# Moving two small parameter loads to an earlier joint, and regrouping the row loads of the last stage

## The chip, the cores and the metric

The kernel runs on one core of one Trainium2 chip, in one launch. The metric is the device time in microseconds (us), as a median over runs. Engines are named as the profile names them: PE (TensorE matmuls) and PEld (its weight loads), DVE (VectorE), ACT (ScalarE), POOL (GpSimd) and SP (SyncE), which computes nothing here and issues most DMAs.

## The reference

Two layers, each a graph attention over a dense 0/1 adjacency matrix followed by a mixture of experts, on 2708 rows of 256 features in float32. What the change touches is the end of layer 1:

```python
def _L1_ffn_ref(x, gate_w, gate_b, w1, b1, w2, b2, gamma, beta):
    gate_logits = x @ gate_w + gate_b                # 16 experts
    topk_vals, topk_idx = jax.lax.top_k(gate_logits, 2)
    topk_w = jax.nn.softmax(topk_vals, axis=-1)
    h = jax.nn.relu(jnp.einsum('bsh,ehf->bsef', x, w1) + b1)
    expert_out = jnp.einsum('bsef,efh->bseh', h, w2) + b2
    sel = jnp.take_along_axis(expert_out, topk_idx[..., None], axis=2)
    y = x + jnp.sum(topk_w[..., None] * sel, axis=2)
    mu, var = jnp.mean(y, -1, keepdims=True), jnp.var(y, -1, keepdims=True)
    return (y - mu) / jnp.sqrt(var + 1e-5) * gamma + beta
...
x = x + _L1_gnn_ref(_layernorm(x), adj, 1, L1_gnn_W_gcn, L1_gnn_W_att, L1_gnn_a_att)
x = x + _L1_ffn_ref(_layernorm(x)[None], ..., L1_ffn_gamma, L1_ffn_beta)[0]
```

gamma and beta are vectors of 256 numbers.

## The kernel before

**Tiles.** The rows are cut into 22 tiles: 20 full ones of 128 rows and two of 74 (`tiles`, `TF`, `TAIL`).

**Stages.** Attention 0 and experts 0 come first, then the preparation of layer 1, attention 1 (its matmuls L1638 run from 719.5 to 872 us), the stream of experts 1 (its last matmul ends at 1112.5 us) and a last stage. Attention 1 and experts 1 are not two loops. `attention`, `points1`, `scatter1`, `experts1.stream` and others are generators, and a planner (`Clock`) with estimated costs lets each emit its next instructions when it thinks that the engine is free. The planner sets the order in which each engine gets its instructions when the kernel is built; on the chip each engine goes through its own list in order and waits for semaphores. `clock.moved(mark, us, latency)` only tells the planner how long a transfer is thought to take.

**The joint behind attention 1.** When the last attention matmul is emitted, `attention` closes the pool `att1`, and calls `late_pools`, which opens the pool `gamma_beta` in the room that `att1` has left and the third set of weight buffers (`room2`). Then SP's list has the loads of experts 1.

**Experts 1.** The router scatters every token's row to two places in a DRAM table `rows_d` (L674, indirect DMAs of POOL), so that rows of one expert lie in pages of 128. `stream` then goes through 45 blocks of 128 rows (`SURE1`). For each block SP issues three DMAs: `load_w1` (L749, 512 KB) and `load_w2` (L753, 512 KB) into one of three buffer sets, and `fetch` (L765, 129.5 KB: the block's rows). A weight load is skipped at run time when the set holds that expert already; the profile then shows it with 0.07 to 0.09 us in place of 0.37 or more. PE runs the matmuls L880 into `hid_ps` (16 by the profile's count), ACT the relu, PE the matmuls L898 into `out_ps` (8), DVE weighs (L904), and POOL adds the block's rows to one of two DRAM tables, `sums1[b % 2]`, by an indirect DMA that accumulates (L909). So even blocks go to table 0 and odd ones to table 1, and block 44, the last, goes to table 0.

`experts1.beside` is `add_beta(b)`, called behind each block. At block 16 it loads gamma and beta, each as one row of 256 numbers repeated over 128 partitions (`broadcast_rows`, L228); from block 20 on it starts one `add_to_x` per block, which adds beta to the rows of `x1` (DVE L1926).

**Early last stage.** `early_last` does the last normalisation of tiles 0 to 5 and 6 to 11 while the stream's final blocks run: it loads both tables' rows (L1420), adds them on POOL (L1953), takes mean and variance on DVE (L427, L428), and applies gamma and the rest (DVE L1963, L1965).

**Last stage.** Behind the stream stands `experts1.rest()`, a conditional block for pages beyond 45, which this input does not enter; its instructions are at L940 and L943. Then `load_y` fetches the rows of `tiles[12:14]`, `[14:16]`, `[16:20]` and `[20:22]` from both tables; `early_out` stores tiles 6 to 11 (L1974); and `last1` does the same sums and normalisation for the late tiles: POOL L1990, DVE L427 and L428, ACT for the root, DVE L2003 and L2005, and the stores L2008. `fetch_rows` issues one DMA for the full tiles of a group (L1420) and one for tiles of 74 rows (L1423).

Of the kernel before, what the change touches and what calls it, by code (L numbers as in the profile page):

```python
# [146 lines left out]
def kernel(  # L147
# [25 lines left out]
    nc = tc.nc  # L173

    ctx.enter_context(tc.manual_schedule(engines={ET.PE, ET.Activation, ET.DVE, ET.SP}))
    N, D = x.shape
# [16 lines left out]
    SURE0, SURE1 = 47, 45  # L193
# [32 lines left out]
    def broadcast_rows(name, src, offset, n, queue=nc.gpsimd, pool=const):  # L226
        tl = pool.tile([P, n], F32, name=name)
        queue.dma_start(  # L228
            tl, bass.AP(tensor=src.tensor, offset=src.offset + offset, ap=[[0, P], [1, n]])
        )  # L230
        return tl
# [275 lines left out]
    def sums_d(name, zero=False):  # L507

        t = dram.tile([W + P, D], F32, name=name)
        lo = 0 if zero else T  # L510
        nc.sync.dma_start(t[lo * P:, :].rearrange("(t p) d -> p t d", p=P),
                          nobody[:, :D].unsqueeze(1).to_broadcast([P, T + 1 - lo, D]))
        return t
# [816 lines left out]
    for step in range(START + T * len(pairs)):  # L1330
# [15 lines left out]
        if step >= START:  # L1346
            k, j = divmod(step - START, T)
# [67 lines left out]
    def fetch_rows(tl, src, group):  # L1415

        full = [t for t, r in group if r == P]
        if full:
            lo = full[0] * P
            ins = nc.sync.dma_start(tl[:, :len(full)], src[lo:lo + len(full) * P, :].rearrange(  # L1420
                "(t p) d -> p t d", p=P))
        if len(full) < len(group):
            ins = nc.sync.dma_start(tl[:TAIL, len(full):], src[TF * P:W, :].rearrange(  # L1423
                "(t p) d -> p t d", p=P)[:TAIL])
        return ins
# [224 lines left out]
    last = pairs[AHEAD - 1]  # L1650
# [5 lines left out]
    for k in range(17):  # L1656
# [8 lines left out]
        if k >= 14:  # L1665
            lo = 4 * (k - 14)
# [25 lines left out]
    sums1 = [sums_d(f"sums1_{k}", zero=k == 1) for k in range(2)]  # L1692
# [11 lines left out]
    clock = Clock()  # L1704
# [34 lines left out]
    def attention():  # L1739
        for i in range(2, T):  # L1740
            acc_slots[i] = yield from acc.get()
            accs[i] = ps_tile("att_ps", "acc")
            for part in range(2):
                yield wide_at[i, part]
                for j in range(part, T, 2):
                    yield "PE", 0.265
                    sum_up(i, j)
                clock.set(wide_slots[i, part])
            clock.start(finish1(*tiles[i]), 0)
        att_scope.close()  # L1750
        late_pools()
        clock.set(started)
# [156 lines left out]
    experts1_scope, last = ExitStack(), {}  # L1909

    def late_pools():
        last["pool"] = ctx.enter_context(tc.tile_pool(name="gamma_beta", bufs=1))
        experts1.pool = experts1_scope.enter_context(tc.tile_pool(name="experts1", bufs=1))
        room = experts1.pool.tile([P, 4 * D * 2], F32, name="room2")
        experts1.add_room(2, room[:, :1024], room[:, 1024:])

    def add_beta(b):
        if b == 16:
            for name, src in (("gamma", L1_ffn_gamma), ("beta", L1_ffn_beta)):
                last[name] = broadcast_rows(name, src, 0, D, nc.sync, last["pool"])  # L1920
        if 20 <= b < 20 + T:
            clock.start(add_to_x(*tiles[b - 20]), 3)

    def add_to_x(t, r):
        yield "DVE", 0.47
        nc.vector.scalar_tensor_tensor(x1[:r, t, :], x1[:r, t, :], common[:r, t:t + 1],  # L1926
                                       last["beta"][:r], op0=OP.add, op1=OP.add)


    y_all = mask_flat.bitcast(F32)[:, :2 * T * D].rearrange(  # L1930
        "p (k t d) -> p k t d", k=2, d=D)
# [40 lines left out]
    def early_out(group):  # L1972
        for (t, _), _ in zip(group[::2], group[1::2]):
            nc.sync.dma_start(of_pair(out, t), y_all[:, 1, t:t + 2])  # L1974

    def load_y(group, mark):
        lo = group[0][0]
        for k in range(2):
            fetch_rows(y_all[:, k, lo:lo + len(group)], sums1[k], group)
        clock.moved(mark, 0.8 * len(group), 2.0)  # L1980

    def last1(group, y_at):

# [39 lines left out]
    clock = Clock()  # L2023

    nc.scalar.preload_act_table_set(LN_TABLE)
    late_last = [tiles[12:14], tiles[14:16], tiles[16:20], tiles[20:22]]
    loads = [Mark() for _ in late_last]
    for group, mark in zip(late_last, loads):
        load_y(group, mark)
    early_out(tiles[6:12])  # L2030
    for group, mark in zip(late_last, loads):
        clock.start(last1(group, mark))
# [32 lines left out]
```

## Time and profile before

| what | us |
|---|---|
| three runs | 1159.67, 1155.14, 1156.15; median 1156.15 |
| the profiled execution | 1157.12 |
| its span, first to last instruction | 1155.4 |
| PE busy | 1030.2 (89% of the span) |
| DVE busy | 542.2 (47%) |
| ACT busy | 573.1 (50%) |
| POOL busy | 366.2 (32%) |

The profile gives one execution. Its span is 1.7 us below that execution's own time. In a line of the trace in order of time the first number is the start in us from the span's start, the second how long the instruction or the run of merged instructions took; "x16" is a count; in brackets at the end is how long the engine stood idle before it, and what ended that. SP's lines are DMA issues: the time is the issuing, not the transfer.

### The profile page before, as it was taken

Reading aid. Unit: us, or ns where it says so; the run is one execution under the profiler, and the core shown is the slowest. Engines: PE = TensorE matmul, PEld = TensorE weight load, DVE = VectorE, ACT = ScalarE, POOL = GpSimd, SP = SyncE. Lnnn points to the kernel's source line nnn. Section 1 sums busy time; section 2 is a strip of 40 time slices with the busy share of each in tenths; the row PEclk is TensorE's granted clock in tenths of the full one; section 3 lists DMA queues with packets and bytes.
Section 4 is the critical chain, followed back from the end, with each engine's and each line's share of the span. In section 5 each row is a group of like instructions: output and inputs, shape, how many; then the busy total and the mean of one; then the engine's idle time right before and its main releaser. Section 6 shows DMA issues by size and latency. Waiting matters only on the chain. (4 is left out here: it accounts for less than half of the span.)

```text
span 1155.4 us, 21226 instructions
## 1 busy us (share of the span) xinstructions
PE 1030.2 (89%) x6665; PEld 914.1 (79%) x6665; DVE 542.2 (47%) x2083; ACT 573.1 (50%) x1599; POOL 366.2 (32%) x417
## 2 busy tenths in 40 slices
PE   5999999997999999999999998998984888899850
PEld 3888888875789999999998954998984777798840
DVE  7678888865531111101111336647776641122368
ACT  4876667653534444444443458446753543344420
POOL 7521121111142221112223351252434355333441
PEclk9999999998999999999999999998996899899985
DMA  9965445410898999999899959401125477787973
GB/s 281 288 236 174 156 159 182 135 77 28 295 283 263 322 322 327 324 304 321 250 318 332 335 155 256 153 1 38 60 65 186 122 180 187 171 214 176 282 196 120
DMA packets 165053, 238.96 MB, mean 207 GB/s; under 512 B 10627, under 2 KB 139966, under 8 KB 162224
## 3 DMA queue, kind: packets, MB, share of 16 engines
q1 hardware_dynamic: 146116, 214.09, 56.6%
q0 software_dynamic: 18816, 23.42, 10.6%
q8 instruction: 56, 0.92, 0.3%
q14 instruction: 65, 0.53, 0.1%
HBM read 205.54 MB, written 54.99 MB: 225 GB/s over the span
## 5 line engine op out<-in xcount | busy, mean ns | idle before, releaser
L904 DVE TENSOR_SCALAR yo<-out_ps,w 128x256 f32<-128x256 f32 x92 | 44.5, 484 | 409.4 <-PE out_ps L898 408.8
L1238 PE MATMUL att_ps<-g_all,z 128*128 128x257 f32 (+3 forms) x968 | 227.3, 388 | 0.0
L1238 PEld LDWEIGHTS att_ps<-g_all,z 128*128 128x128 f32 (+3 forms) x968 | 177.3, 188 | 36.3 <-issue 8.9
L898 PE MATMUL out_ps<-room,ht 128*128 128x256 f32 x872 | 200.0, 381 | 0.0
L880 PEld LDWEIGHTS hid_ps<-xt,room 128*128 128x128 f32 x1504 | 176.2, 193 | 6.3 <-issue 3.4
L880 PE MATMUL hid_ps<-xt,room 128*128 128x128 f32 x1504 | 177.5, 277 | 3.2 <-DMA room<-in_L_ffn_W_dram 2.7
L898 PEld LDWEIGHTS out_ps<-room,ht 128*128 128x128 f32 x872 | 161.9, 191 | 21.0
L1224 ACT ACTIVATE zr<-e_bc,minus_one,g_all 128x256 f32<-128x256 f32 (+3 forms) x242 | 130.5, 591 | 59.0 <-DVE z L1227 58.3
L884 ACT ACTIVATE ht<-hid_ps,w_t 128x128 f32<-128x128 f32 x376 | 128.8, 364 | 26.7 <-PE hid_ps L880 7.4
L909 POOL DMA_INDIRECT sums<-yo,xg x43 | 66.8, 1555 | 233.7 <-DVE side L872 204.7
L674 POOL DMA_INDIRECT rows_d<-xr,place x88 | 92.3, 1049 | 123.7 <-DVE xr L443 77.0
L1638 PE MATMUL att_ps<-half,wide_mask 128*128 128x258 f32 (+1 forms) x968 | 124.5, 290 | 2.5 <-ACT h_all L1575 1.5
L1638 PEld LDWEIGHTS att_ps<-half,wide_mask 128*128 128x128 f32 (+1 forms) x968 | 121.5, 195 | 3.9 <-ACT h_all L1575 2.4
L909 POOL DMA_INDIRECT sums<-yo,xr x45 | 70.7, 1572 | 128.9 <-DVE w L902 42.7
L1227 DVE SCALAR_TENSOR_TENSOR z<-zr,mask_t 128x256 f32<-128x256 f32 (+3 forms) x242 | 96.2, 419 | 30.6 <-ACT zr L1224 17.5
L884 ACT ACTIVATE ht<-hid_ps,w1x 128x128 f32<-128x128 f32 x180 | 62.3, 363 | 95.7 <-PE hid_ps L880 92.5
L874 ACT ACTIVATE w<-xg,side 128x1 f32<-128x1 f32 x43 | 12.7, 294 | 167.5 <-DVE side L872 167.5
L1515 POOL CAST wide_mask<-mask_t 128x1408 fp32r<-128x1408 fp8e4 x31 | 42.5, 1376 | 101.6 <-PE att_ps L1638 67.5
L880 PE MATMUL hid_ps<-lo,wide_mask 128*128 128x128 f32 x480 | 65.7, 294 | 9.9 <-DMA wide_mask<-in_L_ffn_w_dram 9.0
L880 PEld LDWEIGHTS hid_ps<-lo,wide_mask 128*128 128x128 f32 x480 | 62.6, 206 | 13.7 <-issue 10.9
L898 PE MATMUL out_ps<-wide_mask,ht 128*128 128x256 f32 x240 | 60.8, 399 | 0.0
L461 PE MATMUL tr_ps<-ident,xr 128*128 128x128 f32 (+1 forms) x214 | 38.7, 291 | 24.0 <-DMA xr<-rows_d 15.6
(292 smaller groups left out, 1328.3 us busy)
## 6 DMA issues: line engine op xcount, KB each, us to landing
room<-in_L_ffn_W_dram SPq DMA_DIRECT2D x94, 1024.0 KB
wide_mask<-in_L_ffn_w_dram SPq DMA_DIRECT2D x60, 512.0 KB
room<-in_adj_dram SPq DMA_DIRECT2D x20, 1354.0 KB
room<-in_L_ffn_w_dram SPq DMA_DIRECT2D x30, 512.0 KB
rows_d<-nobody SPq DMA_DIRECT2D x1, 7511.0 KB
rows_d<-nobody SPq DMA_DIRECT2D x5, 1295.0 KB
sums<-nobody SPq DMA_DIRECT2D x2, 2944.0 KB
xr<-rows_d SPq DMA_DIRECT2D x45, 129.5 KB
```

The lines of the kernel that those rows point to most:

```text
L461: nc.tensor.transpose(ps[:, c, :r], src[:, c * P:(c + 1) * P], ident[:r, :r])
L674: ins = nc.gpsimd.indirect_dma_start(out=self.rows_d[:, :], in_=self.rows[t][:r], in_offset=None, out_offset=bass.IndirectOffsetOnAxis(ap= ...
L880: nc.tensor.matmul(ps[:, :P], w1_b[:, c, f * P:(f + 1) * P], xt[:, c, :], start=(c == 0), stop=(c == DC - 1))
L884: nc.scalar.activation(ht[:, f, :], ps[:, :P], self.func, bias=self.bias[:, f, b:b + 1])
L898: nc.tensor.matmul(ps[:, :D], ht[:, f, :], self.rooms[b % 3][1][:, f, :], start=False, stop=(f == self.FC - 1))
L904: nc.vector.tensor_scalar(yo, ps[:, :D], w, None, op0=OP.mult)
L909: ins = nc.gpsimd.indirect_dma_start(out=self.sums[k][:, :], in_=yo, in_offset=None, out_offset=bass.IndirectOffsetOnAxis(ap=self.rows.pop ...
L1224: nc.scalar.activation(zr[:k, :n], e_bc[:k, lo:lo + n], AF.Relu, bias=minus_one[:k], scale=g_all[:k, j, D + 1:D + 2])
L1227: nc.vector.scalar_tensor_tensor(z[:k, :n], zr[:k, :n], 1.0, mask_t[:k, j // 2, lo:lo + n, j % 2], op0=OP.add, op1=OP.mult)
L1238: nc.tensor.matmul(accs[i][:r, :D + 1], z[:k, q * P:q * P + r], g_all[:k, j, :D + 1], start=(j == 0), stop=(j == LAST))
L1515: nc.gpsimd.tensor_copy(m, src)
L1638: nc.tensor.matmul(accs[i][:, :D + 2], wide_masks[i, j % 2][:k, j // 2, :], half_k[:k, j, :], start=(j == 0 and half_k is halves[0]), stop ...
```

## The change

Two edits. First, gamma and beta are loaded by `late_pools`, right when the pool `gamma_beta` is opened, instead of by `add_beta` at block 16; both loads stay on SP. Second, in the last stage the loads of both tables no longer alternate group by group: all four groups of the table that does not get the last block's addition come first (`SURE1 % 2` is 1, so table 1), then all four of table 0. The planner is told 0.4 us per tile instead of 0.8, since the mark is set behind the second half alone.

The lists of PE, DVE, ACT and POOL are the same before and after, in content and in order. SP's list differs in these two places: gamma and beta stand between the last `xr<-x_d` loads of attention 1 and the first `where` read and weight load of experts 1, and the eight row loads of the last stage are in the new order.

```diff
     def late_pools():
         last["pool"] = ctx.enter_context(tc.tile_pool(name="gamma_beta", bufs=1))
+        for name, src in (("gamma", L1_ffn_gamma), ("beta", L1_ffn_beta)):
+            last[name] = broadcast_rows(name, src, 0, D, nc.sync, last["pool"])
         experts1.pool = experts1_scope.enter_context(tc.tile_pool(name="experts1", bufs=1))
...
     def add_beta(b):
-        if b == 16:
-            for name, src in (("gamma", L1_ffn_gamma), ("beta", L1_ffn_beta)):
-                last[name] = broadcast_rows(name, src, 0, D, nc.sync, last["pool"])
         if 20 <= b < 20 + T:
             clock.start(add_to_x(*tiles[b - 20]), 3)
...
-    def load_y(group, mark):
+    def load_y(group, k):
         lo = group[0][0]
-        for k in range(2):
-            fetch_rows(y_all[:, k, lo:lo + len(group)], sums1[k], group)
-        clock.moved(mark, 0.8 * len(group), 2.0)
+        fetch_rows(y_all[:, k, lo:lo + len(group)], sums1[k], group)
...
     late_last = [tiles[12:14], tiles[14:16], tiles[16:20], tiles[20:22]]
     loads = [Mark() for _ in late_last]
+
+    for group in late_last:
+        load_y(group, SURE1 % 2)
     for group, mark in zip(late_last, loads):
-        load_y(group, mark)
+        load_y(group, 1 - SURE1 % 2)
+        clock.moved(mark, 0.4 * len(group), 2.0)
     early_out(tiles[6:12])
```

## The prediction

> **What bounds the kernel now.** I read the slices of the page first: PE is busy 89% of the span, so I looked for places in the second half where PE waits, with the waits of PE from 895 us on. The longest wait of PE in the experts is at 997.6 us, 8 us behind the two loads that the change moves. Stretches of 10 us around it (after each engine's busy time: granted clock, DMA share, GB/s):
>
> ```profile
> 980.00:990.00 10.00, 10.00 (x70) 9.34 (x69) 1.39 (x7) 4.41 (x15) 4.19 (x3) 1.00 0.49 79
> 990.00:1000.00 10.00, 7.65 (x54) 6.70 (x52) 1.94 (x9) 3.64 (x12) 3.09 (x2) 1.00 0.98 220
> 1000.00:1010.00 10.00, 7.91 (x42) 7.61 (x43) 0.67 (x3) 2.94 (x10) 2.23 (x2) 0.66 0.66 203
> 1010.00:1020.00 10.00, 10.00 (x70) 9.33 (x69) 2.12 (x8) 4.42 (x15) 3.96 (x3) 1.00 0.68 154
> ```
>
> Between 990 and 1000 the DMA engines are busy 98% of the time and move only 220 GB/s. The trace in order of time says around what:
>
> ```profile
> 988.95 0.39 SPq L749 DMA_DIRECT2D wide_mask<-in_L_ffn_w_dram  x1
> 989.39 0.46 SPq L228 DMA_DIRECT2D gamma<-in_L_ffn_gamma_dram  x1
> 989.90 0.42 SPq L228 DMA_DIRECT2D beta<-in_L_ffn_beta_dram  x1
> 990.74 0.39 SPq L753 DMA_DIRECT2D wide_mask<-in_L_ffn_w_dram  x1
> ...
> 994.06 0.60 SPq L749 DMA_DIRECT2D wide_mask<-in_L_ffn_w_dram  x1
> ...
> 1002.09 3.75 PE L880 MATMUL hid_ps<-lo,wide_mask 128*128 128x128 f32 x16 [4.45 <-DMA wide_mask<-in_L_ffn_w_dram]
> ...
> 1008.35 1.95 PE L880 MATMUL hid_ps<-lo,room 128*128 128x128 f32 x16
> ```
>
> PE waits 4.45 us for the weights issued at 994.06, and then runs its 16 matmuls in 3.75 us in place of 1.95. The DMA view of 989 to 999 us, 40 slots of 0.25 us, shows the moved loads at work: from 992.25 the rate falls from 303 to 20 GB/s and is back above 180 from 994.75, while the engines are busy 60% or more in every slot. 256 KB (2 x 128 rows of 1 KB, all from the same two rows of DRAM) take about 2.7 us. At 346 GB/s, the rate of the joint below, 256 KB would take 0.8 us.
>
> The new place is the joint:
>
> ```profile
> 872.76 0.36 PE L831 MATMUL where_ps<-sel,page_start 58*128 58x8 f32 x2
> 874.52 0.40 SPq L749 DMA_DIRECT2D wide_mask<-in_L_ffn_w_dram  x1
> ...
> 887.00 3.69 SPq L765 DMA_DIRECT2D xr<-rows_d  x4
> 889.11 0.69 PE L461 MATMUL tr_ps<-ident,xr 128*128 128x128 f32 x2 [12.13 <-DMA xr<-rows_d]
> ```
>
> PE waits 12.13 us for the first fetch, which SP holds until the scatters have landed (SP waited 5.7 us on rows_d). From 877 to 886 the DMA share is 0.96: weights and scatters fill it. Before 877 it is 0.30 and 0.47.
>
> The chain that ended last lies in DVE from 1135 us to the end. Its last stage, with POOL:
>
> ```profile
> 1125.40 1.26 POOL L1990 TENSOR_TENSOR mask_t<-mask_t 128x512 f32<-128x512 f32 x1 [3.93 <-DMA mask_t<-sums]
> 1125.52 1.42 DVE L1965 SCALAR_TENSOR_TENSOR mask_t<-mask_t,rstd_y,h_all 128x256 f32<-128x256 f32 x1
> 1135.51 0.43 DVE L427 BATCH_NORM_STATS2 bn<-mask_t 128x6 f32<-128x256 f32 x1 [0.95 <-DVEq L943]
> 1136.28 1.26 POOL L1990 TENSOR_TENSOR mask_t<-mask_t 74x512 f32<-74x512 f32 x1 [2.53 <-DMA mask_t<-sums]
> ```
>
> POOL has the first late pair's sum at 1126.66, DVE takes it at 1135.51: the row loads are not late, DVE is.
>
> [...] from 1133.2 to 1134.6, with only a 74-row load left, the DMA share is 0.14, about 2 of 16. [...] Here a wait of 4.45 us cost the clock (0.66 in the stretch), and waits of 0.71 to 1.71 us did not (2.02 us for 16). [...] Here DVE L1965 takes 1.42 us beside POOL and 0.48 alone.
>
> **Part 1, gamma and beta leave block 16.** SP saves 0.46 + 0.42 us and gaps: the weight load at 994.06 came 5.11 us after the one at 988.95, whereas elsewhere two consecutive real loads stand 4.13 (1022.87, 1027.00), 4.15 (1046.87, 1051.02) and 4.53 us (1071.39, 1075.92) apart. So it would be issued at 993.1 to 993.5. Those second loads were used 5.28 us after issue (hid at 1032.28, wait 0.71), 4.66 (1055.68, 0.10) and 5.51 (1081.43, 1.32), here 8.03. Without the two transfers the matmuls start at 993.2 + 5.3 = 998.5 in place of 1002.09: 3.6 us (3.1 to 4.4). The wait shrinks to about 0.9 us, so the clock stays: from this hid to the next takes 6.26 us now (1002.09 to 1008.35), 3.92 behind the short wait at 1032.28: 2.3 us more. A third load in a row can wait some tenths (0.90 at 1060.66): minus 0.2. The sum is **5.7 us**. Behind it PE has no wait until 1032, and later waits hang on loads that themselves wait for PE, so the gain is carried to the end.
>
> **Part 2, they enter the joint.** On SP they stand before the `where` read and all loads of experts 1, and wait for the last attention matmul, since their room is the attention's. That matmul ends at 872.0; issuing takes 0.9 us, to about 873.1; SP's next step waits for ACT L835 until 873.6 anyway. So on SP they cost nothing; should PE's signal be late, each us would delay the loads by one. On the DMA engines 2.7 us of work start about 2.4 us ahead of the weights, in the share that is free; what spills over pushes weights, scatters and, behind them, the fetch at 887. I take 0.6 us, with 0 and 3 us as ends (3: no head start and some queueing on top). Nothing can be gained here.
>
> **Part 3, the order of the last loads.** It is meant to let table 1's loads start before the last addition has landed. I expect that it does not. The last addition is issued at 1116.20; SP's wait for the first load (5.6 us, on the addition) ends at 1121.62. But at the end of `rest()` POOL stands in INC_SWDGE_SEM (L943, 1.5 us from 1120.06)[...]. [...] So the eight loads go out from 1121.66 as now. The first pair then needs the fifth load, not the second. Ahead of that stand 512 KB more for all engines (1.9 us at the 270 KB/us at which the second and third groups follow now: 1536 KB between 1125.40 and 1131.09), and on two engines also table 1's two tiles of 74 rows: 74 rows of 1 KB per engine, 3.2 us at 24 GB/s each (48 GB/s in the stretch above). So the first sum starts at about 1131 in place of 1125.40 (1125.4 + 1.9 + 3.2, and 0.5 to 1 for the fifth load itself), then at 1132.5, 1133.8, 1135.0, and the tail at about 1136.9.
>
> That costs DVE little and relieves it: four of its steps between 1125 and 1134.6 (1.42, 1.50, 1.49, 1.48 in place of 0.48) lost 4.0 us to POOL's sums. Without them it is done at 1130.6, with the branch at 1131.5, and now waits for POOL: sums there at about 1132.6 and 1133.9, statistics of 1.1 us per pair to 1135.0, the root's mend 0.5, then eight steps of 0.46, of which some three lose up to 1 us to POOL's last sums: done at 1141.3, now 1142.2. **0.9 us** gained (from 1 lost, with the loads later still, to 2 gained). The rest of the chain is DVE's and stays.
>
> **The sum.** -5.7 + 0.6 - 0.9 = -6.0 us. The profiled execution was 1157.12 (span 1155.4 and 1.7 around it), 1.0 above the median of 1156.15; from the median: **1150.2 us**.
>
> **The rivals.** (1) The weights are short anyway: three loads in a row are more than the DMA engines deliver, and the wait stays near 3 us with its clock loss, as at 972.66 (wait 2.91, 16 matmuls in 3.59, no gamma near). Then only 2.5 us go: 1153.4. Against it: around 972 the router's scatters of the last group ran beside, which the runs at 1022, 1046 and 1071 lack. (2) Slower: in the joint the same two rows, read by all engines at once, run at the slot's worst rate, 20 GB/s, beside the scatters: 256 KB in 13 us, less 2.4 head start, 10.7 on the fetch and so on PE. -6.6 + 10.7: 1160.3. From 6.6 us of delay on it decides against the change. The 2.7 us measured speak against it. (3) Part 3 does what it says: POOL's wait covers less than I think, table 1 comes from about 1119, sums earlier by 2.5 us; DVE is the bound, so some 1 us more at best: 1149. (4) The last stage gains nothing and the joint takes 3 us: 1153.4.
>
> **How the numbers follow.** My forecast has 0.70 (own range 1148 to 1152.5), (1) and (4) 0.17 together, (2) 0.06, (3) 0.07. The range 1147.5 to 1154.5 takes in (1), (3) and (4). A measurement of this kernel tells about 0.5% (5.8 us) from no change, so faster begins at 1150.4, in the middle of my own case: 0.51 faster, 0.44 the same, 0.05 slower.
>
> **What would show it.** Right: no wait over 1.5 us behind block 16 and 16 matmuls in about 2.0 us there; gamma and beta issued at 872 to 873 and the first weight load still at 874.5; the fetch at 887 to 888; table 1's first load still behind INC_SWDGE_SEM; POOL's first L1990 some 9 us behind the first row load (now 1121.66 to 1125.40, 3.7). Wrong: a PE wait of 3 us or more with a slow clock near 998, or a fetch behind 890.

## The result, and the profile after

The kernel after took 1151.09 us as a median of 22 runs (1147.67 to 1157.67), the kernel before 1155.62 beside it (22 runs, 1150.15 to 1161.28). The ratio is 0.9959, with a 95% interval of 0.9944 to 0.9974: 4.7 us less, from 3.0 to 6.5. The profiled execution of the kernel after took 1152.47 us, with a span of 1150.8.

That execution is 2.3 us later than the one of before at the end of attention 1 (874.3 against 872.0 us), ahead of anything that the change touches; such offsets differ from execution to execution. So all times below are compared from the last attention matmul or from the last matmul of the experts. At block 17 the two executions happen to be only 0.2 us apart (989.97 and 989.74 us), so the stretches around it can be laid side by side.

The stretches of 10 us around block 16 (length, then busy time and count of PE, PEld, DVE, ACT and POOL, then granted clock, DMA share, GB/s; a packet counts whole in the stretch where it starts, so a share can pass 1), kernel after:

```profile
980.00:990.00 10.00, 10.00 (x70) 9.33 (x69) 1.33 (x6) 4.64 (x15) 4.64 (x3) 1.00 0.53 84
990.00:1000.00 10.00, 9.10 (x66) 8.33 (x65) 2.00 (x9) 4.15 (x15) 4.47 (x3) 1.00 0.95 271
1000.00:1010.00 10.00, 10.00 (x71) 9.39 (x70) 1.73 (x7) 4.90 (x17) 3.26 (x3) 1.00 0.70 174
```

PE is busy 9.10 and 10.00 us where it was busy 7.65 and 7.91, the clock stays at 1.00, and the DMA engines, busy 95% (98% before), move 271 GB/s where they moved 220. The trace there in order of time:

```profile
989.18 0.39 SPq L749 DMA_DIRECT2D wide_mask<-in_L_ffn_w_dram  x1
...
993.36 0.37 SPq L749 DMA_DIRECT2D wide_mask<-in_L_ffn_w_dram  x1
993.81 1.95 PE L880 MATMUL hid_ps<-lo,wide_mask 128*128 128x128 f32 x16
...
998.72 2.02 PE L880 MATMUL hid_ps<-lo,wide_mask 128*128 128x128 f32 x16 [0.90 <-DMA wide_mask<-in_L_ffn_w_dram]
```

The two weight loads stand 4.18 us apart (5.11 before), the matmuls that wait for the second start 5.36 us after its issue (8.03), behind a wait of 0.90 us (4.45), and take 2.02 us (3.75).

The joint, kernel after:

```profile
874.33 0.34 SPq L228 DMA_DIRECT2D gamma<-in_L_ffn_gamma_dram  x1
874.72 0.47 SPq L228 DMA_DIRECT2D beta<-in_L_ffn_beta_dram  x1
...
876.91 0.40 SPq L749 DMA_DIRECT2D wide_mask<-in_L_ffn_w_dram  x1
...
889.57 2.59 SPq L765 DMA_DIRECT2D xr<-rows_d  x3
891.66 0.69 PE L461 MATMUL tr_ps<-ident,xr 128*128 128x128 f32 x2 [12.35 <-DMA xr<-rows_d]
```

Counted from the last attention matmul, the first weight load comes 2.6 us after it (2.5 before), the fetch 15.3 (15.0), and PE's wait is 12.35 us (12.13). The joint costs 0.2 us. In the two stretches of 2.5 us behind the last attention matmul the DMA engines were partly free before,

```profile
872.00:874.50 2.50, 0.58 (x4) 0.52 (x4) 2.26 (x15) 1.37 (x6) 1.89 (x3) 0.87 0.30 106
874.50:877.00 2.50, 1.87 (x8) 1.78 (x8) 2.33 (x10) 0.66 (x2) 1.89 (x3) 0.50 0.47 72
```

and are fuller after:

```profile
874.30:876.80 2.50, 0.58 (x4) 0.52 (x4) 2.26 (x15) 1.32 (x6) 1.88 (x3) 0.89 0.60 93
876.80:879.30 2.50, 1.86 (x8) 1.77 (x8) 2.33 (x10) 0.70 (x2) 1.90 (x2) 0.50 1.00 89
```

The last stage, kernel after:

```profile
1111.40 1.54 POOL L909 DMA_INDIRECT sums<-yo,xr  x1 [0.89 <-SPq L943]
1112.41 4.27 POOL L1952 TENSOR_TENSOR mask_t<-mask_t 128x512 f32<-128x512 f32 x3
1114.28 0.43 DVE L427 BATCH_NORM_STATS2 bn<-mask_t 128x6 f32<-128x256 f32 x1 [5.87 <-POOL mask_t L1952]
1116.65 1.42 SPq L1420 DMA_DIRECT2D mask_t<-sums  x3
1127.44 4.92 POOL L1987 TENSOR_TENSOR mask_t<-mask_t 128x512 f32<-128x512 f32 x4 [10.76 <-DMA mask_t<-sums]
1128.73 0.43 DVE L427 BATCH_NORM_STATS2 bn<-mask_t 128x6 f32<-128x256 f32 x1 [2.93 <-POOL mask_t L1987]
```

The first row load comes 5.25 us behind the issue of the last addition, right when POOL's INC_SWDGE_SEM ends at 1116.68 (5.46 us in the kernel before). The first late sum starts 10.8 us behind that load (3.7 before), and DVE, which had no real wait for POOL there, now has one of 2.93 us. From the last matmul of the experts to the end of the span the kernel after takes 42.86 us and the kernel before 42.90.

### The profile page after: what moved, and what is told of

It reads as the page before. It is cut to its first block, busy times and chain, and to the rows that moved or that the text cites. A ratio compares the mean times of both kernels' runs of the same rounds, so it can differ in the third digit from the quotient of the medians.

```text
span 1150.8 us, 21228 instructions
## 1 busy us (share of the span) xinstructions
PE 1027.6 (89%) x6665; PEld 910.8 (79%) x6665; DVE 541.4 (47%) x2083; ACT 572.9 (50%) x1599; POOL 367.2 (32%) x417
## 3 DMA queue, kind: packets, MB, share of 16 engines
q0 software_dynamic: 18816, 23.42, 10.7%
## 5 line engine op out<-in xcount | busy, mean ns | idle before, releaser
L880 PEld LDWEIGHTS hid_ps<-xt,room 128*128 128x128 f32 x1504 | 176.4, 193 | 6.6 <-issue 3.7
L880 PE MATMUL hid_ps<-xt,room 128*128 128x128 f32 x1504 | 177.7, 277 | 3.5 <-DMA room<-in_L_ffn_W_dram 3.0
L880 PE MATMUL hid_ps<-lo,wide_mask 128*128 128x128 f32 x480 | 62.3, 284 | 5.3 <-DMA wide_mask<-in_L_ffn_w_dram 4.4
L880 PEld LDWEIGHTS hid_ps<-lo,wide_mask 128*128 128x128 f32 x480 | 59.6, 198 | 9.1 <-issue 6.3
```

The lines of the kernel that those rows point to most:

```text
L880: nc.tensor.matmul(ps[:, :P], w1_b[:, c, f * P:(f + 1) * P], xt[:, c, :], start=(c == 0), stop=(c == DC - 1))
```

## The experiments

**One table for all.** Every run left a trace. The columns are us: from the last attention matmul to the first L880 of experts 1 (joint); from that L880 to the one of block 17; from block 17 to block 20, the place of the two loads; from there to the last matmul of the experts; from that to the end. c to f ran once each, where the kernel before took 1184.5 us (one run), and k and l where it took 1176.5. Their six traces share a halt that no other trace has: right behind attention 1, DVE stands idle for 7.6 to 10.5 us, and ACT and SP wait too, for something that the profile calls only "remote". So these six are compared with one another and by stage. All six contain edit 1, and the kernel before was not traced in such runs; whether edit 1 has a part in the halt is open (a and g to j contain it too, and have no halt).

| kernel | joint | 0 to 17 | 17 to 20 | 20 to end of experts | last stage | ratio to before, 95% interval |
|---|---|---|---|---|---|---|
| before | 18.29 | 99.48 | 18.61 | 104.15 | 42.90 | 1 |
| after | 18.52 | 97.16 | 12.67 | 105.25 | 42.86 | 0.9959 (0.9944 to 0.9974) |
| a, edit 1 alone | 18.51 | 96.75 | 13.18 | 105.62 | 43.30 | 0.9964 (0.9946 to 0.9982) |
| b, edit 2 alone | 18.23 | 96.80 | 17.93 | 108.27 | 43.01 | 1.0002 (0.9984 to 1.002) |
| g, after without rest() | 18.49 | 97.40 | 12.31 | 106.65 | 41.80 | 0.9962 (0.9945 to 0.9978) |
| h, a without rest() | 18.41 | 99.02 | 12.58 | 105.10 | 41.34 | 0.996 (0.9941 to 0.998) |
| i, a with late sums on DVE | 18.24 | 96.99 | 13.15 | 103.66 | 45.08 | 0.999 (0.9972 to 1.0007) |
| j, a with early sums on DVE | 18.79 | 99.26 | 12.42 | 105.16 | 39.31 | 0.9904 (0.9876 to 0.9931) |
| c, hot rows again at block 16 | 26.28 | 103.99 | 15.35 | 105.22 | 42.17 | one run |
| d, 256 different rows there | 26.49 | 106.11 | 14.40 | 105.87 | 42.89 | one run |
| e, two single rows there | 26.49 | 105.76 | 14.08 | 106.02 | 42.48 | one run |
| f, four more hot loads in the joint | 33.87 | 104.49 | 13.28 | 105.16 | 42.94 | one run |
| k, all late and early sums on DVE | 24.32 | 104.46 | 14.11 | 106.85 | 42.78 | 0.9981 (0.996 to 1.0002) |
| l, after with early sums on DVE | 26.53 | 105.35 | 13.07 | 103.85 | 42.61 | 0.9989 (0.9972 to 1.0005) |

**a and b: each edit alone.** a is the kernel before with the first two hunks of the diff, b the kernel before with the rest.

> Edit 1 alone (gamma and beta in the joint, the old order of the last loads). Theory (the two loads at block 16 make the wait, the last stage's order is worth nothing): all of the gain, 4 to 6 us below before, ratio about 0.995; PE's wait near 998 us at most 1.5 us with 16 matmuls in about 2.0 us; from DVE's first L427 of the early last stage (behind POOL L1953) to its last step 32.8 us, as before. Rival (the order of the last loads brings a part): 2 us or less remains here, ratio above 0.997.

> Edit 2 alone (gamma and beta at block 16, the new order of the last loads). Theory: no difference, ratio 0.999 to 1.001; PE's wait near 998 us back at 4 to 5 us with a slow clock behind it; the first row load still leaves SP when POOL's INC_SWDGE_SEM ends; DVE takes 32 to 33.5 us from its first L427 to its last step, having lost no time beside POOL but having waited about 3 us for POOL's first late sum. Rival (the order is the gain): ratio 0.996 or so.

Edit 1 alone took 1152.61 us (15 runs) and edit 2 alone 1156.99 (14), the kernel before 1157.0 (28). So the whole gain is that of edit 1, within the intervals. The trace of b has block 16 as in the kernel before, with a wait of 3.19 us where 4 to 5 were expected:

```profile
1000.17 3.75 PE L880 MATMUL hid_ps<-lo,wide_mask 128*128 128x128 f32 x16 [3.19 <-DMA wide_mask<-in_L_ffn_w_dram]
```

**c, d and e: what in the two loads costs.** Each is the kernel after with two more loads at block 16, into spare tiles: gamma and beta once more (c); or the same 256 KB from 256 different rows of x (d); or one row each (e). The diff shows the three edits below one another; each run has one of them.

```diff
     def add_beta(b):
+        if b == 16:
+            for k, src in enumerate((L1_ffn_gamma, L1_ffn_beta)):                        # c
+                broadcast_rows(f"spare{k}", src, 0, D, nc.sync, last["pool"])
+            for k in range(2):                                                           # d
+                nc.sync.dma_start(last["pool"].tile([P, D], F32, name=f"spare{k}"),
+                                  x[k * P:(k + 1) * P, :])
+            for k in range(2):                                                           # e
+                nc.sync.dma_start(last["pool"].tile([P, D], F32, name=f"spare{k}")[:1],
+                                  x[k:k + 1, :])
```

> The changed kernel, and at block 16 again two loads of gamma and beta by SP into two spare tiles that nobody reads: 256 KB, each row repeated over 128 partitions. Theory (repeated rows hold the DMA engines for about 2.7 us): PE's wait behind block 16 is back at 4 to 5 us, 16 matmuls behind it in over 3 us, and about 6 us are lost. Rival (the place in the program made the wait, or chance): wait at most 1.5 us.

> As c_hot16, but the two extra loads at block 16 read 256 different rows of 1 KB (of the input x) into the same spare tiles: the same bytes, descriptors and issues. Theory (it is that all 128 descriptors of a load read one row): the two loads pass in about 0.8 us, PE waits 1.5 to 2.8 us, clearly less than in c_hot16. Rival (256 KB more in the queue and two more issues are enough, the repeated row doesn't matter): the wait is 4 to 5 us as in c_hot16.

> As c_hot16, but the two extra loads at block 16 bring one row of 1 KB each to one partition: SP issues as much, the DMA engines move almost nothing. Theory: only SP's 0.9 us delay of the next weight loads is left, PE waits 1 to 2 us and keeps its clock. If SP's delay were most of the cost: 3 us or more.

They took 1178.16, 1177.69 and 1175.74 us, one run each. Runs of one kernel spread over 11 us (the kernel before in the result above: 1150.15 to 1161.28), so these times don't rank them. The stretches of 1 us tell more. In c, the second and third us in which the two added loads are at the front of the queue:

```profile
1017.00:1018.00 1.00, 1.00 (x8) 0.93 (x7) 0.35 (x1) 0.00 (x0) 0.00 (x0) 1.00 0.21 46
1018.00:1019.00 1.00, 1.00 (x11) 1.00 (x10) 0.31 (x3) 0.82 (x4) 0.59 (x1) 1.00 0.45 140
```

and in d, at the same distance behind the weight load ahead of them:

```profile
1016.00:1017.00 1.00, 0.90 (x5) 0.50 (x4) 0.24 (x1) 0.00 (x0) 0.00 (x0) 1.00 0.97 324
1017.00:1018.00 1.00, 1.00 (x10) 1.00 (x10) 0.43 (x3) 0.40 (x2) 0.48 (x1) 1.00 1.14 320
```

With the hot rows (one row read 128 times) the rate falls to 46 GB/s; in d no stretch of 1 us from 1014 to 1019 us is below 211. The engines need not count as busy meanwhile: their share is 0.21 in c, and 0.24 at 69 GB/s in b (993 to 994 us), but 0.98 at 45 GB/s in the kernel before (993 to 994 us). The low rate is what these have in common; why the share differs is open. The weights behind the two loads reach PE 7.21 us after their issue in c, 4.20 in d and 4.75 in e (8.03 and 6.74 in before and b). The gap between the two weight loads on SP is 5.02, 5.12 and 5.12 us, alike in all three, and 4.18 without them: that part of the cost, 0.9 us, is the two issues and not the data. From block 17 to 20 the three take 15.35, 14.40 and 14.08 us; f and l, which have nothing there in the same kind of run, take 13.28 and 13.07, though k took 14.11. So c lost about 2 us against f and l and not the 6 expected, with a wait of 3.58 us and not 4 to 5. The longest wait is 1.79 us in d and 1.24 in e, as expected. With one run each and k at 14.11, the stage times alone don't separate d and e from no load at all; the rates and the arrival of the weights carry the argument.

One thing in c came otherwise than in before and b: the matmuls behind its wait ran at the full clock.

```profile
1025.04 2.02 PE L880 MATMUL hid_ps<-lo,wide_mask 128*128 128x128 f32 x16 [3.58 <-DMA wide_mask<-in_L_ffn_w_dram]
```

**f: how full the joint is.** The kernel after with four more loads of gamma behind beta in the joint.

```diff
             last[name] = broadcast_rows(name, src, 0, D, nc.sync, last["pool"])
+        for k in range(4):
+            broadcast_rows(f"spare{k}", L1_ffn_gamma, 0, D, nc.sync, last["pool"])
```

> The changed kernel with four more loads of gamma, repeated over 128 partitions, behind the two in the joint, into spare tiles that nobody reads: 768 KB in place of 256 KB, 1.9 us more of issues. Theory (the head start before the weights is about used up by two loads, so more lands on the fetch that PE waits for): from the last attention matmul to the first tr_ps matmul of experts 1, now 17.4 us (17.1 before the change), grows by 4 to 7 us. Rival (the joint has room): it grows by less than 1.5 us.

It took 1180.16 us. The joint is 33.87 us against 26.28 to 26.53 in c, d, e and l (24.32 in k, whose halt is the shortest): 7.4 us for 512 KB more, a little over the 4 to 7 expected, and nearly nothing of it hidden. DMA share and GB/s in the joint of f:

```profile
896.00:898.00 2.00, 0.00 (x0) 0.00 (x0) 1.69 (x12) 0.00 (x0) 0.00 (x0) 0.50 1.01 77
898.00:900.00 2.00, 0.00 (x0) 0.00 (x0) 1.49 (x10) 0.21 (x1) 0.00 (x0) 0.50 1.01 70
```

and of e in the same place:

```profile
896.00:898.00 2.00, 0.00 (x0) 0.00 (x0) 1.73 (x11) 0.00 (x0) 0.00 (x0) 0.50 0.94 311
```

All 16 engines busy at 70 to 77 GB/s: at that rate a hot load of 128 KB takes 1.7 to 1.9 us. The four cost 1.85 each. But f has the halt, in which POOL issued the last scatters: with SP's list free again nothing held the fetch but the loads ahead of it (it comes 7.4 us behind gamma in e and 13.0 in f), where in the kernel after SP waits for the scatters and the fetch comes 15.2 us behind gamma. So f tells the price of a hot load that nothing hides. In the kernel after two of them, some 3.5 us at that rate, cost 0.2 us; how many more would fit there was not measured.

**g and h: is it rest() that holds the last loads?** The kernel after, and a, without the call of `rest()`, whose block this input does not enter.

```diff
     clock.run()
-    experts1.rest()
     experts1_scope.close()
```

> The kernel after, with the call of rest() taken out; that is the conditional block for blocks past the sure ones, which this input does not enter, so nothing that it computes here is missing. Theory (the prediction's reading): the wait of POOL at the head of that block (INC_SWDGE_SEM, L943, which ended at 1116.68 us in the kernel after) is what keeps the first row load of table 1 from going ahead of the last addition. Then, with the block gone, the first row load of table 1 starts 2.5 to 4 us closer to the end of the experts' last matmul than in the kernel after (there 14.5 us after it), about when the last but one addition has landed; POOL's first late sum starts some 2 to 3 us earlier too, DVE's wait of 2.9 us for it falls below 1 us, and the time falls by 1.5 to 3 us against the kernel after, that is to a ratio of 0.9932 to 0.9948 against the kernel before. Rival (the block costs nothing: the loads come behind the last addition's own landing anyway): the first row load starts within 0.7 us of the same place and the ratio stays 0.996.

> Edit 1 alone (gamma and beta in the joint, loads of the last stage in the order of the kernel before) with the call of rest() taken out, the block which this input does not enter. In this order the first load is of the table that the last addition goes to, so it waits for that addition whatever the block does. Theory (the block's wait is the last addition's landing and little more): the first row load starts 0.3 to 1.5 us earlier against the end of the experts' last matmul than with edit 1 alone, and since DVE has early rows to work on until long after, the time falls by 0 to 1 us: ratio against the kernel before 0.995 to 0.9965. If the block itself is worth more (its register loads and branches on five engines, and the ACT table load behind it), 1 to 2.5 us less: ratio 0.994 or below.

In the text for g, 14.5 us is a slip: in the kernel after the first row load comes 8.76 us after the experts' last matmul. In g it comes 5.1 us after it, 3.7 earlier; in h 6.7, in a 9.0, so 2.3 earlier. So the block does hold both tables' loads, and by more in h than expected. That within the block it is INC_SWDGE_SEM is read from the times alone (it ends at 1116.68 us in the kernel after, where the first row load is issued at 1116.65, and at 1121.66 in the kernel before, where that load is issued at 1121.66), since the whole block was taken out; how it would hold them was the author's assumption and is not shown. In g DVE has no wait for the first late sum any more, as expected. But the time hardly follows: the last stage is 1.1 us shorter in g than in the kernel after and 2.0 in h than in a, and the ratios, 0.9962 and 0.996, are those of the kernels with the block. The gain expected for g (0.9932 to 0.9948) was not there.

**i: the late sums on DVE.** a, with the five pair sums of `last1` on DVE.

```diff
-            yield "POOL", 1.3
-            nc.gpsimd.tensor_tensor(y_all[:r, 0, t:t + 2], ...)
-            yield "DVE", 1.3
+            yield "DVE", 1.9
+            nc.vector.tensor_tensor(y_all[:r, 0, t:t + 2], ...)
```

> Edit 1 alone, with the five pair sums of the late tiles done by DVE instead of POOL. Theory (DVE is the bound of the last stage and is slowed by POOL's sums beside it: steps of 0.48 us alone took 1.37 to 1.57 us where a sum of POOL of 1.3 us lay beside them): DVE takes on five sums of about 1 us each, 5 us in all, and is rid of four to seven slowed steps of 0.9 us each and of its waits for POOL, 5 to 8 us; the tail of DVE, 33.2 us with edit 1 alone, becomes 30.5 to 33 us, and the time falls by 0 to 2.5 us: ratio 0.994 to 0.9965. Rival (the slowed steps are no contention with POOL but with the row loads that land in the same buffers): the slowed steps stay, the tail grows by 3 to 5 us, ratio 0.999 to 1.001.

It took 1152.79 us. All steps of DVE beside the sums are now 0.47 to 0.49 us (up to 1.57 in a), so the slowing came with POOL's sums, and a sum takes 0.66 to 0.69 us on DVE; its tail is 32.21 us against 33.20 in a. But the planner now puts the 74-row tiles last, and from DVE's last step to the end of the span it takes 6.37 us instead of 3.61: the last stage is 1.8 us longer. The ratio is that of the rival, the mechanism is not.

**j: the early sums on DVE.** a, with the sums of tiles 6 to 11 on DVE.

```diff
-            yield "POOL", 1.3
-            nc.gpsimd.tensor_tensor(y_all[:, 0, t:t + 2], y_all[:, 0, t:t + 2],
-                                    y_all[:, 1, t:t + 2], OP.add)
+            yield ("DVE", 1.0) if lo else ("POOL", 1.3)
+            adder = nc.vector if lo else nc.gpsimd
+            adder.tensor_tensor(y_all[:, 0, t:t + 2], y_all[:, 0, t:t + 2],
+                                y_all[:, 1, t:t + 2], OP.add)
```

> Edit 1 alone, with the three pair sums of the early tiles 6 to 11 done by DVE instead of POOL. Theory: what starts DVE's tail is not the row loads but POOL's three early sums (L1952, 4.3 us), which in POOL's order stand behind the last addition of the experts, so that DVE stands idle for 6 us after its last step for the experts (5.97 us with edit 1 alone, 5.87 us in the kernel after). With the sums on DVE (three of about 1 us) its first statistics start 3 to 4.5 us earlier against the end of the experts' last matmul (now 6.5 us after it); the late rows then bound part of the tail, since their last sum on POOL ends 25 us after that matmul whatever is done before it, so that 1.5 to 4 us are left: ratio against the kernel before 0.993 to 0.995. Rival (the late rows are the bound already): the first statistics start earlier, the tail of DVE grows by as much, ratio 0.996 to 0.997.

This is the fastest of all, and better than expected: 1144.79 us (6 runs) where the kernel before took 1154.93 (59 runs), and 5 us below g and h, which ran beside it; its interval lies wholly below that of a. DVE's view, in order of time:

```profile
1105.54 1.28 DVE L1953 TENSOR_TENSOR mask_t<-mask_t 128x512 f32<-128x512 f32 x2
...
1107.38 0.68 DVE L1953 TENSOR_TENSOR mask_t<-mask_t 128x512 f32<-128x512 f32 x1
1107.98 0.42 DVE L427 BATCH_NORM_STATS2 bn<-mask_t 128x6 f32<-128x256 f32 x1
...
1121.43 0.43 DVE L427 BATCH_NORM_STATS2 bn<-mask_t 128x6 f32<-128x256 f32 x1 [2.26 <-POOL mask_t L1990]
```

The sums lie between DVE's steps for the last two blocks, the tail starts 1.0 us after the experts' last matmul instead of 6.5, and takes 34.65 us instead of 33.20, because DVE then waits for the late rows (2.26 and 1.95 us). The trace shows 4.0 us less in the last stage than in a; the middles of the two ratios, 0.9904 and 0.9964, are 6.9 us apart, with intervals that take in 4.

**k and l: more of it, and the two edits with it.** k is j with the late sums on DVE too and the 74-row tiles as the second late group, l is the kernel after with j's edit.

```diff
-    late_last = [tiles[12:14], tiles[14:16], tiles[16:20], tiles[20:22]]
+    late_last = [tiles[12:14], tiles[20:22], tiles[14:16], tiles[16:20]]
```

> Edit 1 alone, with all pair sums of tiles 6 to 21 done by DVE, and the pair of 74 rows (tiles 20 and 21) as the second of the late groups instead of the last. Theory: with the early sums alone on DVE the tail starts 1.0 us after the experts' last matmul but takes 34.65 us, of which 4.2 us are waits for POOL's first two late sums and some 4.5 us are five steps slowed beside POOL's sums; on DVE a sum took 0.68 us, so five cost 3.4 us. The tail becomes 32.5 to 34 us, and nothing comes after it but the last store, 3.6 us with 128 rows in it (6.4 us where the 74 rows came last). Ratio against the kernel before 0.988 to 0.9905, 0 to 2 us below the kernel with the early sums alone on DVE. Rival: the 74 rows, loaded second, hold up the loads behind them, DVE waits for the last group instead, the tail is 35 us or more, ratio 0.991 to 0.993.

> The kernel after (both edits), with the three pair sums of tiles 6 to 11 on DVE. It tells what edit 2 does once the tail of DVE starts early. Theory (edit 2 puts the four loads of one table ahead of every load of the other, so that the first late pair is whole only 8 to 11 us after the first row load, not 3 to 4): DVE is through with its early tiles some 17 to 18 us after the experts' last matmul and then waits for the first late sum until 24 to 26 us after it, 6 to 9 us in all (4.2 us in two waits with the loads in their old order); the gain of the early sums shrinks from 0.6% to 0.1 to 0.35% beyond edit 1: ratio against the kernel before 0.9925 to 0.9955. Rival (edit 2 is neutral wherever the tail starts): the ratio is that of edit 1 with the early sums on DVE, 0.9904, within 0.0015.

k: 1174.87 us (22 runs), l: 1174.85 (22), the kernel before beside them 1176.52 (43). In k the 74 rows cost time, as in the rival: DVE waits 5.39 us for them, SP's four issues behind theirs take 5.90 us (six took 2.99 in j), and the DMA engines are little used for a while (DMA share and GB/s last in the stretches):

```profile
1148.36 0.69 DVE L1990 TENSOR_TENSOR mask_t<-mask_t 74x512 f32<-74x512 f32 x1 [5.39 <-DMA mask_t<-sums]
```

```profile
1140.00:1141.00 1.00, 0.00 (x0) 0.00 (x0) 0.42 (x1) 0.00 (x0) 0.00 (x0) 0.50 0.12 33
1141.00:1142.00 1.00, 0.00 (x0) 0.00 (x0) 0.89 (x2) 0.00 (x0) 0.00 (x0) 0.50 0.17 56
```

A share of 0.12 is as much as 2 of 16 engines (16 x 0.12 = 1.9); in the kernel before it was 0.14 where only a 74-row load was left. In l DVE is through with its early tiles, and waits:

```profile
1147.06 4.92 POOL L1988 TENSOR_TENSOR mask_t<-mask_t 128x512 f32<-128x512 f32 x4 [14.11 <-DMA mask_t<-sums]
1148.35 0.43 DVE L427 BATCH_NORM_STATS2 bn<-mask_t 128x6 f32<-128x256 f32 x1 [8.13 <-POOL mask_t L1988]
```

8.1 us in one wait against 4.2 in two in j: with its order of loads edit 2 takes back what j's edit brings (last stage 42.61 us against 39.31 in j and 42.86 in the kernel after). The ratios of k and l lie above what was expected even so, and both intervals take in 1: in these runs no gain can be made out, though both kernels contain edit 1. With the halt, the two loads stand ahead of weights and fetch with no wait for scatters to hide behind, so edit 1 may be worth less there; it was not run alone in such runs, so this stays open.

## Why the prediction was right

**The sum.** Forecast were 6.0 us less, measured 4.7 (3.0 to 6.5); the median of 1151.09 lies 0.9 above the forecast of 1150.2. The stages of the two traces give 5.3 us less (5.55 less, 0.23 more and 0.0 in the three parts below). The forecast lay just beyond the bound of 0.5% and the result just within it, at a ratio of 0.9959: of the two, "faster" had been given 0.51 and "the same" 0.44. The case expected, with the mechanism of its first two parts, is the one that came.

**Part 1 was right in mechanism and size.** Blocks 17 to 20 take 18.61 and 17.93 us with the loads at block 16 (before, b) and 12.31 to 13.18, on average 12.72, in the six kernels without (after, a, g to j): 5.55 us, forecast 5.7. The matmuls behind the wait start 3.6 us earlier, as worked out (8.75 us behind block 17's first matmul, 12.35 before), and the clock term is 2.34 us in the pair of profiled executions (6.26 against 3.92 from one L880 to the next). That nothing is given back later fits: the rest of the experts takes 103.7 to 106.7 us without the loads there, 104.2 and 108.3 with them. That the rows are hot was only inferred in the prediction; the rates of d against c and of f against e show it, in one trace each.

**The clock term came, but by luck.** c waited 3.58 us and kept the clock, b waited 3.19 and lost it. In each of the 14 traces, all changes of the granted clock lie whole multiples of 3.41 us apart (in the kernel before at 972.84, 976.25, 1000.14 and 1006.97 us). These steps, carried on over the waits, for the kernel before, for b and two for c (first PE's busy time; the clock is third from the end):

```profile
996.73:1000.14 3.41, 0.92 (x5) 0.46 (x3) 0.67 (x3) 0.00 (x0) 0.00 (x0) 1.00 0.98 305
```

```profile
996.02:999.43 3.41, 0.95 (x5) 0.50 (x3) 0.67 (x3) 0.00 (x0) 0.38 (x1) 1.00 1.05 328
```

```profile
1019.90:1023.31 3.41, 1.55 (x8) 1.02 (x6) 0.67 (x3) 0.18 (x1) 0.06 (x1) 1.00 1.05 333
1023.31:1026.72 3.41, 1.68 (x15) 1.71 (x16) 0.00 (x0) 0.88 (x4) 1.55 (x1) 1.00 1.11 343
```

In the kernel before and in b 2.5 us of the wait lie in one step, PE is busy 0.92 and 0.95 us in it, and at its end the clock fell, before the wait was over. In c the longer wait lies across a border, PE is busy 1.55 and 1.68 us in the two steps, and the clock stayed. So the length of a wait, by which alone the prediction went, does not tell whether the clock falls: 3.58 us in c kept it, and 3.19 us in b and 2.91 us in the kernel before (up to 972.66; the clock fell at 972.84, and PE was busy 0.50 us in the step that ended there) lost it. What differs between them is how they lay on the steps. That this decides is not shown: in the kernel before the clock also fell at 904.57 us, behind a step (from 901.15) in which the profile shows PE busy throughout. The 2.3 us of the clock came in the profiled execution, where the wait lay as it did; in how many executions it does so was not counted. Without the clock loss the change is worth some 2 us (15.35 us in c against 13.07 and 13.28 in l and f, one trace each, less 0.2 in the joint).

**Part 2 was right, its size smaller.** The joint costs 0.23 us (18.49 on average in the six against 18.26 in before and b), forecast 0.6. The transfers were longer than the 2.7 us assumed: some 3.5 us at f's rate. That they cost less all the same fits the free DMA share: it rose from 0.30 and 0.47 to 0.60 and 1.00 in the 5 us behind the last attention matmul, and what PE waits for is the fetch, for which SP still waits on the scatters (5.3 us at the longest, 5.7 before). Rival (2), 10.7 us on the fetch, did not come.

**Part 3 had the mechanism and missed the value.** Table 1's loads did not start early (rival 3 fell), and g and h showed that the block of `rest()` is what holds them. The term "0.9 us gained" is the step that failed: it measured 0.0. Its sum has an error: ahead of the fifth load stand not "512 KB more" but 768, the second and third groups of table 1 (two and four tiles of 128 KB). At the same 270 KB/us that is 0.95 us more, as much as the whole gain. The first late sum came 10.8 us behind the first row load and not 9.3, so that DVE waited 2.93 us where I had 1.1. Its early steps did lose their collisions with POOL (none above 0.49 us until the wait, four of them before), and the wait gave that back. The view that I did not use was DVE's idle time before its first L427 of the tail, in the kernel before

```profile
1119.07 0.43 DVE L427 BATCH_NORM_STATS2 bn<-mask_t 128x6 f32<-128x256 f32 x1 [6.05 <-POOL mask_t L1953]
```

behind POOL's three early sums (5.87 us in the kernel after): that, and not the row loads, set when the tail could begin, as j showed.

**Rivals 1 and 4.** Behind block 16 the wait is 0.00 to 1.38 us in the six kernels, so the weights are not short there (1 falls). Of 4 one half held, the last stage gained nothing; the joint did not take 3 us.

## What to carry to other kernels

A small parameter that is one DRAM row spread over all partitions was not a small transfer here (128 KB a load, at 70 to 77 GB/s in f): price it by the rate that the trace shows for it, and put it where PE waits for something else anyway (two cost 0.2 us in the joint, where PE waits 12 us); where nothing hid it, it cost its full time (1.85 us for each of f's four). Before reordering the loads of a last stage, ask which engine starts late there and behind what; here three sums that stood behind the last addition in POOL's list were worth about as much as both edits (4.0 us in j's trace on top of edit 1), as long as the loads keep their old order. Ask not only how long PE waits but where the wait lies among the steps of 3.41 us at which the granted clock changed here (c kept it over 3.58 us, b lost it in 3.19). Compare by stage anchors when executions drift by more than the effect.

## What the runs showed of the hardware that I had not expected

- Loads that read one DRAM row of 1 KB 128 times ran at 62 to 77 GB/s with all 16 DMA engines busy (f, 896 to 902 us), against 311 to 393 GB/s in e in that place, and at 46 GB/s with a share of 0.21 in c.
- Within a trace, the changes of the granted clock lay whole multiples of 3.41 us apart (all 14). In before and b it fell about 2.5 us into the wait, at 1000.14 and 999.43 us, with PE idle since 997.6 and 997.0; in c it did not fall at all in 3.58 us.
- A sum of 128x512 in float32 took 0.68 us on DVE (j) and 1.26 on POOL (before).
- From DVE's last step to the end of the span it took 6.4 us where the last store had two 74-row tiles (i), and 3.6 where it had two 128-row tiles (a).
